# Cross-attention and feed-forward on one core: context as 128 rows and 64 paired rows, projections in front of the scores

## The chip, the cores and the metric

The kernel runs on one core of a Trainium2 chip. The metric is the time of one execution on the device in microseconds (us). One execution was also recorded by the hardware profiler; the profile and the trace below are of that one.

## What is computed

One block of a transformer on `x` (2048 rows of 256) with a context of 1601 rows of 192, in fp32. Shortened from the reference (`g_norm`, `g_out` scale the layer norms inside; all mask entries are true in the inputs, but the kernel handles any mask):

```python
q = layer_norm(layernorm(x), g_norm) @ Wq          # 16 heads of 64
k, v = split(context @ Wkv)                        # 16 heads of 64 each
k, v = concat([null_k, k]), concat([null_v, v])    # 1602 keys
sim = (q * 64**-.25) @ (k * 64**-.25).T
sim = where(mask, sim, -big)                       # null key always kept
x = x + layer_norm((softmax(sim) @ v) @ Wout, g_out)
h = [xn, -xn], xn = layernorm(x)
x = x + s2 * (2 relu(s1 * (2 relu(s0 * h @ W0)) @ W1)) @ W2    # W = +1 or -1
```

## The kernel before

The context comes transposed (192 rows, one column per key). It lies in one tile `ctx_sb` of 96 rows and two halves, so that each projection is two accumulating fp32 matmuls over 96 rows.

**Units.** The 16 heads are taken as 8 pairs `p` (64 + 64 = 128 partitions), the 2048 queries as 4 blocks `b` of 512. The main loop (L463) runs over 32 units `(p, b)`, pair outermost. The keys are cut in 13 tiles of 128 (the last of 66), and for the maxima in four chunks of 402 and 400.

**One unit**, in the order in which the loop issues it (the order is written by hand; every engine takes its own instructions in that order):

1. Scores. For each key tile, `exps` (L284) adds two 64-row matmuls, one for each head, into one of two PSUM buffers that live through the whole unit. The keys were made into steps beforehand: from tile 2 on a tile holds its difference to the tile 256 keys earlier (`keys_stepped`, L216, on POOL), so that each matmul turns the buffer into the next scores. The first two tiles also subtract a row maximum, `mT`, by a matmul with ones (L307). ACT takes the exponential (L309), POOL adds the exponentials into `acc` (L498, L500). Between the tiles stand 16 `max_chunk` (L251) of the *next* unit: TensorE makes cheaper fp32r scores from `kr` and `qr`, DVE reduces them to maxima (L262). After the last, `max_combined` (L264).
2. Values. 26 matmuls `weighted` (L312) into `av`. After the third tile, `divided` (L331) works for the *previous* unit: TensorE sums `acc` by a matmul with ones (`den`), DVE takes the reciprocal and multiplies (`aoT`, L336, L337).
3. The end of the unit: ACT copies `av` (L542). Then, in blocks 0 to 2, projections of the next pair follow: `project_v` and `project_k`, as the table `ahead` (L371) shares them out: block 0 two value groups and key chunk 0, block 1 two value groups and key chunk 1, block 2 key chunks 2 and 3 and then `keys_stepped`. Then `project_out` of the previous unit (`po`, added into `y_sb` on DVE, L329), `max_turned` of the next unit (a transpose on TensorE, then `mT` on DVE, L274), and `project_q` two units ahead (`psq`, read by ACT as `qr` and `qT`, L197 and L198).

In `project_k` DVE multiplies by the mask (`kT`, L211) and adds the null key where the mask drops one (`kr`, L212). `project_v` is read by ACT (L238); DVE puts in the null value (L242).

**PSUM** is handed out in turns from two pools of two 1024-column buffers: `spare` (the two score buffers, `av`, `po`) and `flex` (the rest). A buffer is free when its last reader is done.

**The opening** (L373 to L460) makes pair 0 itself: loads on the SP, ACT and POOL queues, the normalised input for blocks 0 and 1, all keys and values of pair 0, the first maxima. `fan` (L447), a 128x512 tile of ones times `pick`, is made there for `max_turned`. In units 0 and 1 the loop prepares the input of blocks 2 and 3 in between (L513 and L544): statistics on DVE, normalisation on ACT (`centred_beside`, L134), eight transposes on TensorE. The feed-forward layers (L566 to L656) follow the units.

Of the kernel before, what the change touches and what calls it, by code (L numbers as in the profile page):

```python
# [9 lines left out]
F32 = mybir.dt.float32  # L10
# [3 lines left out]
ALU = mybir.AluOpType  # L14
# [6 lines left out]
KEYS = M + 1  # L21
CD = 192
HEADS, DH = 16, 64
INNER = HEADS * DH
FF = 1024
NP = HEADS // 2
# [9 lines left out]
def xattn_ffn(ctx, tc, x, ctxT, mask, g_norm, null_kv, wq, wkv, wout, g_out, k0, k1, k2, s0, s1, s2, out):  # L36
    nc = tc.nc
# [8 lines left out]
    def flex(name):  # L46
        return ps_f.tile([128, 2, 512], F32, tag="f", name=name)
# [95 lines left out]
    with ExitStack() as att:  # L143
# [2 lines left out]
        ep = att.enter_context(tc.tile_pool(name="exps", bufs=KC))  # L146
        wp = att.enter_context(tc.tile_pool(name="work", bufs=2))

        ctx_sb = ap.tile([96, 2, KEYS], F32, name="ctx_sb")
        gn_sb = ap.tile([128, 2], F32, name="gn_sb")  # L150
        nullk = ap.tile([128, 1], F32, name="nullk")
        nullv = ap.tile([1, 128], F32, name="nullv")
# [3 lines left out]
        maskb = ap.tile([128, KC], F32, name="maskb")  # L156
        ones_r = ap.tile([128, 128], F32R, name="ones_r")
        mcol = ap.tile([128, 128], F32, name="mcol")
        fan = ap.tile([128, 4, 128], F32, name="fan")
        pick = ap.tile([128, 4], F32, name="pick")  # L160

        weights = {}

        def load_pair(p):
            wq_t = pp.tile([128, 2, 128], F32, tag="wq", name=f"wq_{p}")
            wkv_t = pp.tile([96, 2, 2, 128], F32, tag="wkv", name=f"wkv_{p}")
            wo_t = lp.tile([128, D], F32, tag="wo", name=f"wo_{p}")
            for kv in range(2):
                nc.sync.dma_start(
                    out=wkv_t[:, :, kv, :],  # L170
                    in_=wkv[:, ds(kv * INNER + 128 * p, 128)].rearrange("(c r) w -> r c w", c=2),
                )
                if kv == 0:
                    if p == 0:
                        load_x(0)
                    nc.sync.dma_start(out=wq_t, in_=wq[:, ts(p, 128)].rearrange("(c r) w -> r c w", c=2))
            nc.sync.dma_start(out=wo_t, in_=wout[ts(p, 128), :])
            weights[p] = (wq_t, wkv_t, wo_t)


        pairs, queries = {}, {}
# [16 lines left out]
            nc.scalar.mul(qT, ps[:, 0, :], DH**-0.5)  # L198
            queries[p, b] = (qT, qr)

        def project_k(p, n, get=flex):
            kT, _, kr = pairs[p]
            start, w = CHUNKS[n]
            keys = ds(start, w)
            ps = get(f"psk_{p}_{n}")
            for c in range(2):
                nc.tensor.matmul(  # L207
                    ps[:, 0, :w], weights[p][1][:, c, 0, :], ctx_sb[:, c, keys], start=c == 0, stop=c == 1
                )

            nc.vector.tensor_tensor(kT[:, keys], ps[:, 0, :w], keep[:, keys], ALU.mult)  # L211
            nc.vector.scalar_tensor_tensor(kr[:, keys], drop[:, keys], nullk[:, 0:1], kT[:, keys], ALU.mult, ALU.add)  # L212
            if n == 0:
                nc.vector.tensor_copy(kT[:, 0:1], nullk)

        def keys_stepped(p):  # L216

            kT = pairs[p][0]
            for at in range(256 * ((KEYS - 1) // 256), 0, -256):
                w = min(256, KEYS - at)  # L220
                nc.gpsimd.tensor_tensor(kT[:, ds(at, w)], kT[:, ds(at, w)], kT[:, ds(at - 256, w)], ALU.subtract)

        def project_v(p, n, get=flex):
            v = pairs[p][1]
            tiles = range(4 * n, min(4 * n + 4, KC))
            rows = 128 if n < 3 else KLAST
            ps = get(f"psv_{p}_{n}")
            for i, t in enumerate(tiles):
                for c in range(2):
                    nc.tensor.matmul(  # L230
                        ps[:rows, 0, ts(i, 128)],
                        ctx_sb[:, c, ds(128 * t, rows)],
                        weights[p][1][:, c, 1, :],
                        start=c == 0,
                        stop=c == 1,
                    )
            w = len(tiles)
            nc.scalar.copy(  # L238
                v[:rows, ds(4 * n, w), :], ps[:rows, 0, : 128 * w].rearrange("p (t d) -> p t d", d=128)
            )  # L240
            if n == 0:
                nc.vector.tensor_copy(v[0:1, 0, :], nullv)  # L242

# [25 lines left out]
        def max_turned(p, b):  # L269

            ps = flex(f"mt_{p}_{b}")
            nc.tensor.transpose(ps[:, 0, :128], mcol, ident)
            shifts[p, b] = wp.tile([128, 512], F32R, tag="mT", name=f"mT_{p}_{b}", bufs=1)
            nc.vector.tensor_tensor(  # L274
                shifts[p, b].rearrange("p (t q) -> p t q", t=4),
                ps[:, 0:1, :128].to_broadcast([128, 4, 128]),
                fan,
                ALU.mult,
            )

        def rows_of(k):
            return 128 if k < KC - 1 else KLAST
# [37 lines left out]
        def project_out(p, b, aoT):  # L320
            po = spare(f"po_{p}_{b}")
            pv = po.rearrange("p a (c d) -> p (a c) d", d=D)
            for t in range(4):
                nc.tensor.matmul(pv[:, t, :], aoT[:, ts(t, 128)], weights[p][2], start=True, stop=True)  # L324
            y = y_sb[:, ts(b, 4), :]
            if p == 0:
                nc.vector.tensor_copy(y, pv)
            else:
                nc.vector.tensor_tensor(y, pv, y, ALU.add)  # L329
# [38 lines left out]
        units = [(p, b) for p in range(NP) for b in range(NB)]  # L368
        extra = {0, 4, 8}

        ahead = {0: ((0, 1), (0,)), 1: ((2, 3), (1,)), 2: ((), (2, 3)), 3: ((), ())}  # L371

        begin = tc.manual_schedule()  # L373
        begin.__enter__()

        def load_x(b):
            nc.sync.dma_start(out=x_sb[:, ts(b, 4), :], in_=x[ts(b, 512), :].rearrange("(c p) d -> p c d", p=128))
# [4 lines left out]
        for n, (at, w) in enumerate(CHUNKS):  # L382
            skip = 1 if n == 0 else 0
            nc.scalar.dma_start(
                out=ctx_sb[:, :, ds(at + skip, w - skip)],
                in_=ctxT[:, ds(at + skip - 1, w - skip)].rearrange("(c r) k -> r c k", c=2),
            )
        nc.gpsimd.memset(eps2_sb, EPS * EPS)
        nc.gpsimd.memset(eps_sb, EPS)
        make_identity(nc, ident)  # L390
        nc.gpsimd.memset(keep[:, 0:1], 0)
        nc.gpsimd.memset(ctx_sb[:, :, 0:1], 0.0)
        nc.gpsimd.dma_start(out=keep[:, 1:], in_=mask.partition_broadcast(128))
        nc.gpsimd.dma_start(out=gn_sb, in_=g_norm.rearrange("(c p) -> p c", p=128))
        for j in range(2):
# [16 lines left out]
        nc.gpsimd.memset(mcol, 0.0)  # L412
        nc.gpsimd.memset(maskb, 0.0)
        nc.gpsimd.memset(ones, 1.0)
        nc.gpsimd.memset(fan, 1.0)

        nc.scalar.activation(warm, eps_sb, AF.Sqrt)

        open_pair(0)
        xn = input_root(0)  # L420
        nc.vector.tensor_scalar(ones_r, ident, 0.0, 1.0, ALU.mult, ALU.add)
        nc.vector.tensor_tensor(pick, ident[:, 0:4], ident[:, DH : DH + 4], ALU.add)
        input_normed(0, *xn)
        project_k(0, 0, slot)
        input_turned(0, slot)
        project_k(0, 1, slot)
        project_q(0, 0, slot)
        for t in range(4):
            max_chunk(0, 0, 4 * t, slot)
            if t == 1:  # L430
                project_k(0, 2, slot)
        for t in range(4):
            max_chunk(0, 0, 4 * t + 1, slot)
            if t == 1:
                project_k(0, 3, slot)
                keys_stepped(0)
        xn = input_root(1)
        input_normed(1, *xn, beside=True)
# [4 lines left out]
        nc.vector.tensor_scalar(  # L443
            maskb[:KLAST, KC - 1 : KC], mcol_u8[:KLAST, KC - 1 : KC], -MASKED, MASKED, ALU.mult, ALU.add
        )
        for t in range(4):
            nc.vector.tensor_scalar_mul(fan[:, t, :], fan[:, t, :], pick[:, t : t + 1])  # L447
        for n in (2, 3):
            for t in range(4):
                max_chunk(0, 0, 4 * t + n, slot)  # L450
                if n == 2 or t == 3:
                    if t % 2 == 1:
                        project_v(0, (0, 1)[t // 2] if n == 2 else 2, slot)
# [5 lines left out]
        project_v(0, 3)  # L459
        begin.__exit__(None, None, None)  # L460
        last = None
        with tc.manual_schedule():
            for u, (p, b) in enumerate(units):  # L463
# [232 lines left out]
```

## Time and profile before

| | us |
|---|---|
| median of 3 runs (1351.82 to 1353.6) | 1353.06 |
| the profiled execution | 1355.55 |
| its span, first to last instruction | 1353.7 |
| TensorE busy / its share | 1329.3 / 98% |
| DVE, ACT, POOL busy | 880.7, 607.7, 994.8 |
| opening, up to the first unit | 51.4 |
| the 32 units, up to the last one's first score | 1081.8 |
| mean granted TensorE clock | 0.992 |

How to read the rows shown below. Each names the line of the kernel, the engine, the operation, the tiles as out<-in, their shapes, and a count. PE is TensorE and PEld its weight loads, DVE VectorE, ACT ScalarE, POOL GpSimd, SP the queue of most loads. In a timeline the first two numbers are the start and the duration in us, with like instructions of one engine merged; in brackets stands how long the engine was idle before and what ended that. In groups, the numbers after the bar are busy us in all, mean ns of one, and idle us before. A matmul's recorded duration contains its way through the array, so neighbours overlap; the time that one costs is read from start to start.

### The profile page before, as it was taken

Reading aid. Unit: us, or ns where it says so; the run is one execution under the profiler, and the core shown is the slowest. Engines: PE = TensorE matmul, PEld = TensorE weight load, DVE = VectorE, ACT = ScalarE, POOL = GpSimd, SP = SyncE. Lnnn points to the kernel's source line nnn. Section 1 sums busy time; section 2 is a strip of 40 time slices with the busy share of each in tenths; the row PEclk is TensorE's granted clock in tenths of the full one; section 3 lists DMA queues with packets and bytes.
Section 4 is the critical chain, followed back from the end, with each engine's and each line's share of the span. In section 5 each row is a group of like instructions: output and inputs, shape, how many; then the busy total and the mean of one; then the engine's idle time right before and its main releaser. Section 6 shows DMA issues by size and latency. Waiting matters only on the chain.

```text
span 1353.7 us, 16255 instructions
## 1 busy us (share of the span) xinstructions
PE 1329.3 (98%) x6528; PEld 664.6 (49%) x6528; DVE 880.7 (65%) x957; ACT 607.7 (45%) x655; POOL 994.8 (73%) x492
## 2 busy tenths in 40 slices
PE   6999999999999999999999999999999999999998
PEld 3544444444444444444444444444444443688887
DVE  5677776676667756686767656767676884464431
ACT  1666454445444454444544454454445557421220
POOL 4377987798888987798779877987798999711100
PEclk9799999999999999999999999999999999999999
DMA  5000000000000000000000000000000010000000
GB/s 136 4 1 7 0 1 8 8 1 0 8 1 7 1 1 8 7 1 1 7 8 1 1 8 8 0 1 5 0 16 1 1 39 0 1 0 16 16 16 16
DMA packets 14940, 12.31 MB, mean 9 GB/s; under 512 B 2240, under 2 KB 14784, under 8 KB 14864
## 3 DMA queue, kind: packets, MB, share of 16 engines
q1 hardware_dynamic: 13552, 9.70, 2.5%
q10 hardware_dynamic: 832, 1.23, 0.3%
q8 instruction: 51, 0.84, 0.3%
q0 software_dynamic: 480, 0.34, 0.1%
q14 instruction: 25, 0.20, 0.1%
HBM read 9.17 MB, written 2.10 MB: 8 GB/s over the span
## 4 chain that ended last, share of the span: by engine, by line
PE 93%; DVE 3%; ACT 2%; DMA 1%; issue 0%; POOL 0%; SPq 0%; ACTq 0%
PE sT L296 28%; PE av L316 27%; PE ps L592 10%; PE max L259 8%; PE psq L196 4%; PE po L324 4%; PE psv L230 3%; PE psk L207 3%; PE ps L615 2%; PE den L334 2%; ACT e L309 1%; PE sT L307 1%; DVE mx L262 1%; DMA x_sb<-in_x 1%; PE xT L361 0%
## 5 line engine op out<-in xcount | busy, mean ns | idle before, releaser
L500 POOL TENSOR_TENSOR acc<-acc,e 128x1024 f32<-128x1024 f32 (+1 forms) x352 | 847.3, 2407 | 27.6
L262 DVE TENSOR_REDUCE mx<-max 128x2 f32<-128x800 f32 (+1 forms) x512 | 481.3, 988 | 70.9 <-PE max L259 61.2
L309 ACT ACTIVATE e<-sT,maskb 128x1024 f32<-128x1024 f32 (+1 forms) x416 | 460.0, 1115 | 64.0 <-PE sT L296 38.0
L296 PE MATMUL sT<-qT,kT 64*128 64x512 f32 (+1 forms) x1664 | 444.4, 612 | 1.6 <-ACT e L309 1.4
L316 PE MATMUL av<-e,v 128*64 128x512 f32 (+1 forms) x1664 | 369.5, 594 | 1.0
L259 PE MATMUL max<-kr,qr 64*128 64x400 f32 (+1 forms) x1024 | 285.7, 568 | 2.3 <-DVE mx L262 1.5
L316 PEld LDWEIGHTS av<-e,v 128*64 128x64 f32 (+1 forms) x1664 | 116.7, 137 | 239.0 <-issue 219.3
L259 PEld LDWEIGHTS max<-kr,qr 64*128 64x128 f32 x1024 | 97.3, 186 | 187.2 <-DVE mx L262 149.7
L296 PEld LDWEIGHTS sT<-qT,kT 64*128 64x128 f32 (+1 forms) x1664 | 135.3, 181 | 104.8 <-ACT e L309 81.5
L498 POOL TENSOR_TENSOR acc<-e,e 128x1024 f32<-128x1024 f32 x32 | 75.5, 2358 | 147.6 <-ACT e L309 147.6
L542 ACT COPY avs<-av 128x512 f32<-128x512 f32 x32 | 18.8, 587 | 327.0 <-PE av L316 327.0
L336 DVE RECIPROCAL aoT<-den 128x512 f32<-128x512 f32 x31 | 104.1, 3357 | 70.0 <-PE den L334 70.0
L197 ACT ACTIVATE qr<-psq 128x512 fp32r<-128x512 f32 x32 | 19.1, 597 | 139.1 <-PE psq L196 139.1
L592 PE MATMUL ps<-h0hi,w 128*128 128x512 f32 x256 | 79.5, 392 | 0.0
L592 PE MATMUL ps<-h0lo,w 128*128 128x512 f32 x256 | 78.9, 389 | 0.0
L211 DVE TENSOR_TENSOR kT<-psk,keep 128x400 f32<-128x400 f32 (+1 forms) x32 | 18.4, 574 | 90.0 <-PE psk L207 89.8
L119 POOL TENSOR_TENSOR y_sb<-y_sb,gout_sb 128x256 f32<-128x256 f32 x12 | 9.3, 776 | 90.1 <-DVE y_sb L86 90.1
L581 DVE SCALAR_TENSOR_TENSOR h1lo<-ps,h1hi 128x1024 fp32r<-128x1024 f32 x16 | 19.6, 1224 | 69.0 <-ACT h1hi L580 69.0
L196 PE MATMUL psq<-xnT,wq 128*128 128x512 f32 x128 | 62.2, 610 | 0.6 <-DVE kT L211 0.6
L324 PE MATMUL po<-wo,aoT 128*128 128x256 f32 x256 | 61.5, 383 | 0.0
L329 DVE TENSOR_TENSOR y_sb<-po,y_sb 128x1024 f32<-128x1024 f32 x28 | 34.2, 1220 | 40.0 <-PE po L324 39.8
L580 ACT ACTIVATE h1hi<-ps 128x1024 fp32r<-128x1024 f32 x16 | 16.4, 1027 | 94.6 <-PE ps L592 94.6
(125 smaller groups left out, 1054.8 us busy)
## 6 DMA issues: line engine op xcount, KB each, us to landing
x_sb<-in_x SPq DMA_DIRECT2D x4, 512.0 KB, 8.7
out_x<-o SPq DMA_DIRECT2D x8, 256.0 KB, 2.1
wkv<-in_wkv SPq DMA_DIRECT2D x16, 96.0 KB, 2.1
wq<-in_wq SPq DMA_DIRECT2D x8, 128.0 KB, 2.3
wo<-in_wout SPq DMA_DIRECT2D x8, 128.0 KB, 2.1
xnT<-in_k SPq DMA_DIRECT2D x1, 1024.0 KB, 5.9
ctx_sb<-in_ctxT ACTq DMA_DIRECT2D x3, 300.0 KB, 7.9
xnT<-in_k SPq DMA_DIRECT2D x1, 512.0 KB, 3.9
```

Source lines behind the costliest of these rows:

```text
L196: nc.tensor.matmul(ps[:, 0, :], weights[p][0][:, c, :], xnT[:, b, c, :], start=c == 0, stop=c == 1)
L207: nc.tensor.matmul(ps[:, 0, :w], weights[p][1][:, c, 0, :], ctx_sb[:, c, keys], start=c == 0, stop=c == 1)
L259: nc.tensor.matmul(ps[:, j, :w], queries[p, b][1][rows, ts(t, 128)], pairs[p][2][rows, ds(start, w)], start=True, stop=True)
L262: nc.vector.tensor_reduce(maxima[p, b][:, t, :, c], ps[:, :, :w], AX.X, ALU.max)
L296: nc.tensor.matmul(ps[:n, j, :], kT[rows, ds(128 * k, n)], qT[rows, :], start=k < 2, stop=k >= 2, skip_group_check=k >= 2,)
L309: nc.scalar.activation(e[:n], ps[:n], AF.Exp, bias=maskb[:n, k : k + 1])
L316: nc.tensor.matmul(av[ts(j, DH), 0, :], v[:n, k, ts(j, DH)], e[:n, j, :], start=k == 0, stop=k == KC - 1)
L324: nc.tensor.matmul(pv[:, t, :], aoT[:, ts(t, 128)], weights[p][2], start=True, stop=True)
L336: nc.vector.reciprocal(aoT, ps)
L498: nc.gpsimd.tensor_tensor(acc, es[0], es[1], ALU.add)
L500: nc.gpsimd.tensor_tensor(acc[:m], acc[:m], es[k][:m], ALU.add)
L592: nc.tensor.matmul(ps[:, f, :], w(c)[:, ts(2 * g + f, 128)], parts[part][:, c, :], start=i == 0, stop=i == len(steps) - 1,)
```

## The change

- The context is held as `ctx_a` (rows 0 to 127) and `ctx_b` (rows 128 to 191, 64 rows). `ctx_b` has the 64 rows twice, in partitions 0 to 63 and again in 64 to 127; the weights `wa`, `wb` likewise. A projection is then one matmul over 128 rows and one over 64 rows, and the 64-row ones of two chunks or tiles are issued side by side in the two halves of the array, each into its own PSUM bank.
- The opening keeps undivided matmuls for pair 0 (`first_keys`, `first_values`): `ctx_b` and `wb` have zeros in the second half there. In unit 0 the second copy of the rows is loaded, and both context tiles are multiplied by the mask once on DVE, so that keys of later pairs need no mask of their own.
- `project_k` and `project_v` make half the keys or half the values of a pair at a time: blocks 0 and 1 the keys, blocks 2 and 3 the values. They stand last in a unit, behind `max_turned`, `project_out` and `project_q`, right in front of the next unit's scores. `max_turned` comes first. `keys_stepped` runs in block 1.
- ACT writes `kT` and DVE writes `kr` straight from PSUM, each engine beginning with the other's second chunk ("crosswise"). The null key and null value columns go in on POOL.
- `fan` is gone; `mT` is the turned maxima times a broadcast `pick`.

```diff
-        ctx_sb = ap.tile([96, 2, KEYS], F32, name="ctx_sb")
+        ctx_a = ap.tile([128, KEYS], F32, name="ctx_a")
+        ctx_b = ap.tile([128, KEYS], F32, name="ctx_b")
...
-        fan = ap.tile([128, 4, 128], F32, name="fan")
-        pick = ap.tile([128, 4], F32, name="pick")
+        pick = ap.tile([128, 4, 1], F32, name="pick")
...
         def load_pair(p):
             wq_t = pp.tile([128, 2, 128], F32, tag="wq", name=f"wq_{p}")
-            wkv_t = pp.tile([96, 2, 2, 128], F32, tag="wkv", name=f"wkv_{p}")
+            wa_t = pp.tile([128, 2, 128], F32, tag="wa", name=f"wa_{p}")
+            wb_t = pp.tile([128, 2, 128], F32, tag="wb", name=f"wb_{p}")
             wo_t = lp.tile([128, D], F32, tag="wo", name=f"wo_{p}")
-            for kv in range(2):
-                nc.sync.dma_start(
-                    out=wkv_t[:, :, kv, :],
-                    in_=wkv[:, ds(kv * INNER + 128 * p, 128)].rearrange("(c r) w -> r c w", c=2),
-                )
-                if kv == 0:
-                    if p == 0:
-                        load_x(0)
-                    nc.sync.dma_start(out=wq_t, in_=wq[:, ts(p, 128)].rearrange("(c r) w -> r c w", c=2))
+            both = wkv.rearrange("r (k w) -> r k w", k=2)[:, :, ts(p, 128)]
+            nc.sync.dma_start(out=wa_t, in_=both[0:128])
+            nc.sync.dma_start(out=wb_t[:64], in_=both[128:CD])
+            if p == 0:
+                nc.gpsimd.memset(wb_t[64:], 0.0)
+                load_x(0)
+            else:
+                nc.sync.dma_start(out=wb_t[64:], in_=both[128:CD])
+            nc.sync.dma_start(out=wq_t, in_=wq[:, ts(p, 128)].rearrange("(c r) w -> r c w", c=2))
             nc.sync.dma_start(out=wo_t, in_=wout[ts(p, 128), :])
-            weights[p] = (wq_t, wkv_t, wo_t)
+            weights[p] = (wq_t, wa_t, wb_t, wo_t)
...
+        def project_k(p, m):
+            kT, _, kr = pairs[p]
+            start, w = ((0, 401), (802, 400))[m]
+            ps = flex(f"psk_{p}_{m}")
+            for i in range(2):
+                nc.tensor.matmul(
+                    ps[:, i, :w], weights[p][1][:, 0, :], ctx_a[:, ds(start + i * w, w)], start=True, stop=False
+                )
+            for i in range(2):
+                rows = ts(i, 64)
+                nc.tensor.matmul(
+                    ps[:, i, :w], weights[p][2][rows, 0, :], ctx_b[rows, ds(start + i * w, w)], start=False, stop=True
+                )
+            for i in range(2):
+                keys, other = ds(start + i * w, w), ds(start + (1 - i) * w, w)
+                nc.scalar.copy(kT[:, keys], ps[:, i, :w])
+                nc.vector.scalar_tensor_tensor(
+                    kr[:, other], drop[:, other], nullk[:, 0:1], ps[:, 1 - i, :w], ALU.mult, ALU.add
+                )
+            if m == 0:
+                nc.gpsimd.tensor_copy(kT[:, 0:1], nullk)
...
+        def first_values(n, get):
+            v = pairs[0][1]
...
+                keys = ds(128 * t, rows)
+                out_t = ps[:rows, 0, ts(i, 128)]
+                nc.tensor.matmul(out_t, ctx_a[:, keys], weights[0][1][:, 1, :], start=True, stop=False)
+                nc.tensor.matmul(out_t, ctx_b[:, keys], weights[0][2][:, 1, :], start=False, stop=True)
...
+        def project_v(p, m):
+            v = pairs[p][1]
+            ps = flex(f"psv_{p}_{m}")
+            pv = ps.rearrange("p i (t d) -> p (i t) d", d=128)
+            tiles = range(8 * m, min(8 * m + 8, KC))
+            for t in tiles:
+                n = rows_of(t)
+                nc.tensor.matmul(
+                    pv[:n, t - 8 * m, :],
+                    ctx_a[:, ds(128 * t, n)],
+                    weights[p][1][:, 1, :],
+                    start=t % 4 == 0,
+                    stop=False,
+                    skip_group_check=True,
+                )
+            for t in sorted(tiles, key=lambda t: (t % 4, t)):
+                n = rows_of(t)
+                rows = ts((t - 8 * m) // 4, 64)
+                nc.tensor.matmul(
+                    pv[:n, t - 8 * m, :],
+                    ctx_b[rows, ds(128 * t, n)],
+                    weights[p][2][rows, 1, :],
+                    start=False,
+                    stop=True,
+                    skip_group_check=True,
+                )
+            if m == 0:
+                nc.scalar.copy(v[:, 0:8, :], pv)
+                nc.gpsimd.tensor_copy(v[0:1, 0, :], nullv)
+            else:
+                nc.scalar.copy(v[:, 8:12, :], pv[:, 0:4, :])
+                nc.scalar.copy(v[:KLAST, 12, :], pv[:KLAST, 4, :])
...
-                fan,
+                pick.to_broadcast([128, 4, 128]),
...
-        ahead = {0: ((0, 1), (0,)), 1: ((2, 3), (1,)), 2: ((), (2, 3)), 3: ((), ())}
...
             nc.scalar.dma_start(
-                out=ctx_sb[:, :, ds(at + skip, w - skip)],
-                in_=ctxT[:, ds(at + skip - 1, w - skip)].rearrange("(c r) k -> r c k", c=2),
+                out=ctx_a[:, ds(at + skip, w - skip)], in_=ctxT[0:128, ds(at + skip - 1, w - skip)]
+            )
+            nc.scalar.dma_start(
+                out=ctx_b[:64, ds(at + skip, w - skip)], in_=ctxT[128:CD, ds(at + skip - 1, w - skip)]
             )
...
-        nc.gpsimd.memset(ctx_sb[:, :, 0:1], 0.0)
+        nc.gpsimd.memset(ctx_a[:, 0:1], 0.0)
+        nc.gpsimd.memset(ctx_b[:64, 0:1], 0.0)
+        nc.gpsimd.memset(ctx_b[64:], 0.0)
...
-        nc.gpsimd.memset(fan, 1.0)
...
-        project_k(0, 0, slot)
+        first_keys(0, slot)
...
-        for t in range(4):
-            nc.vector.tensor_scalar_mul(fan[:, t, :], fan[:, t, :], pick[:, t : t + 1])
...
+                if u == 0:
+                    nc.sync.dma_start(out=ctx_b[64:, 1:], in_=ctxT[128:CD, :])
+                    for part in (ctx_a, ctx_b):
+                        nc.vector.tensor_tensor(part, part, keep, ALU.mult)
...
                 if u < 2:
                     input_turned(u + 2)
-                if p + 1 < NP:
-                    for n in ahead[b][0]:
-                        project_v(p + 1, n, spare if n % 2 else flex)
-                    for n in ahead[b][1]:
-                        project_k(p + 1, n, spare if n % 2 else flex)
-                    if b == 2:
-                        keys_stepped(p + 1)
+                if nxt is not None:
+                    max_turned(*nxt)
                 if nxt is None:
                     uT = turned(0)
                 if last is not None:
                     project_out(*last[:2], aoT)
-                if nxt is not None:
-                    max_turned(*nxt)
                 if u + 2 < len(units):
                     project_q(*units[u + 2])
+                if p + 1 < NP:
+                    (project_k if b < 2 else project_v)(p + 1, b % 2)
+                    if b == 1:
+                        keys_stepped(p + 1)
                 last = (p, b, avs, acc)
```

Left out: `first_keys` and `first_values` are the former `project_k` and `project_v` with `ctx_a`, `ctx_b` and their weights over 128 rows each, called at the same places of the opening; `project_out` takes `weights[p][3]`.

More of the change, by code (lines that the diff above doesn't have):

```diff
@@ L199, in project_q, with first_keys @@
             queries[p, b] = (qT, qr)
-        def project_k(p, n, get=flex):
-            kT, _, kr = pairs[p]
+        def first_keys(n, get):
+            kT, _, kr = pairs[0]
             start, w = CHUNKS[n]
             keys = ds(start, w)
[L205 to L209, printed above, removed]
+            ps = get(f"psk_0_{n}")
+            nc.tensor.matmul(ps[:, 0, :w], weights[0][1][:, 0, :], ctx_a[:, keys], start=True, stop=False)
+            nc.tensor.matmul(ps[:, 0, :w], weights[0][2][:, 0, :], ctx_b[:, keys], start=False, stop=True)
             nc.vector.tensor_tensor(kT[:, keys], ps[:, 0, :w], keep[:, keys], ALU.mult)
@@ L221, in keys_stepped @@
                 nc.gpsimd.tensor_tensor(kT[:, ds(at, w)], kT[:, ds(at, w)], kT[:, ds(at - 256, w)], ALU.subtract)
-        def project_v(p, n, get=flex):
-            v = pairs[p][1]
+        def first_values(n, get):
+            v = pairs[0][1]
             tiles = range(4 * n, min(4 * n + 4, KC))
             rows = 128 if n < 3 else KLAST
-            ps = get(f"psv_{p}_{n}")
+            ps = get(f"psv_0_{n}")
             for i, t in enumerate(tiles):
[L229 to L236, printed above, removed]
+                keys = ds(128 * t, rows)
+                out_t = ps[:rows, 0, ts(i, 128)]
+                nc.tensor.matmul(out_t, ctx_a[:, keys], weights[0][1][:, 1, :], start=True, stop=False)
+                nc.tensor.matmul(out_t, ctx_b[:, keys], weights[0][2][:, 1, :], start=False, stop=True)
             w = len(tiles)
@@ L323, in project_out @@
             for t in range(4):
-                nc.tensor.matmul(pv[:, t, :], aoT[:, ts(t, 128)], weights[p][2], start=True, stop=True)
+                nc.tensor.matmul(pv[:, t, :], aoT[:, ts(t, 128)], weights[p][3], start=True, stop=True)
             y = y_sb[:, ts(b, 4), :]
@@ L421, in xattn_ffn @@
         nc.vector.tensor_scalar(ones_r, ident, 0.0, 1.0, ALU.mult, ALU.add)
-        nc.vector.tensor_tensor(pick, ident[:, 0:4], ident[:, DH : DH + 4], ALU.add)
+        nc.vector.tensor_tensor(pick[:, :, 0], ident[:, 0:4], ident[:, DH : DH + 4], ALU.add)
         input_normed(0, *xn)
-        project_k(0, 0, slot)
+        first_keys(0, slot)
         input_turned(0, slot)
-        project_k(0, 1, slot)
+        first_keys(1, slot)
         project_q(0, 0, slot)
@@ L430, in xattn_ffn @@
             if t == 1:
-                project_k(0, 2, slot)
+                first_keys(2, slot)
         for t in range(4):
@@ L434, in xattn_ffn @@
             if t == 1:
-                project_k(0, 3, slot)
+                first_keys(3, slot)
                 keys_stepped(0)
@@ L452, in xattn_ffn @@
                     if t % 2 == 1:
-                        project_v(0, (0, 1)[t // 2] if n == 2 else 2, slot)
+                        first_values((0, 1)[t // 2] if n == 2 else 2, slot)
                 if n == 3 and t == 1:
@@ L458, in xattn_ffn @@
         max_turned(0, 0)
-        project_v(0, 3)
+        first_values(3, flex)
         begin.__exit__(None, None, None)
```

## The prediction

> **What bounds the kernel now.** I read the page first: its busy shares, its slices, its chain.
>
> ```profile
> PE 1329.3 (98%) x6528; PEld 664.6 (49%) x6528; DVE 880.7 (65%) x957; ACT 607.7 (45%) x655; POOL 994.8 (73%) x492
> PE   6999999999999999999999999999999999999998
> PE 93%; DVE 3%; ACT 2%; DMA 1%; issue 0%; POOL 0%; SPq 0%; ACTq 0%
> PE sT L296 28%; PE av L316 27%; PE ps L592 10%; PE max L259 8%; PE psq L196 4%; PE po L324 4%; PE psv L230 3%; PE psk L207 3%; PE ps L615 2%; PE den L334 2%; ACT e L309 1%; PE sT L307 1%; DVE mx L262 1%; DMA x_sb<-in_x 1%; PE xT L361 0%
> ```
>
> TensorE is busy in every slice but the opening, and the chain is TensorE for 93% of the span. So an instruction taken off it should shorten the span, if its stage has no other limit. Next the TensorE timeline at the end of a unit (pair 4, block 0), where the edit lies; columns are start, duration, name, count:
>
> ```profile
> 643.58 3.84 PE L230 MATMUL psv<-wkv,ctx_sb 96*128 96x128 f32 x32
> 647.25 1.51 PE L207 MATMUL psk<-ctx_sb,wkv 96*128 96x402 f32 x4
> 648.61 1.89 PE L324 MATMUL po<-wo,aoT 128*128 128x256 f32 x8
> 650.34 0.27 PE L272 MATMUL mt<-ident,mcol 128*128 128x128 f32 x1
> 650.44 1.88 PE L196 MATMUL psq<-xnT,wq 128*128 128x512 f32 x4
> 652.26 1.13 PE L296 MATMUL sT<-qT,kT 64*128 64x512 f32 x4
> ```
>
> Starts follow each other with no hole: here TensorE alone sets the time. An fp32 matmul is two recorded passes (psv x32 is 8 tiles by 2 halves by 2). Now all engines at the start of the next stage, the scores:
>
> ```profile
> 613.10 1.88 PE L196 MATMUL psq<-xnT,wq 128*128 128x512 f32 x4
> 614.91 1.13 PE L296 MATMUL sT<-qT,kT 64*128 64x512 f32 x4
> 615.08 0.60 ACT L197 ACTIVATE qr<-psq 128x512 fp32r<-128x512 f32 x1 [3.22 <-PE psq L196]
> 616.38 1.11 ACT L309 ACTIVATE e<-sT,maskb 128x1024 f32<-128x1024 f32 x1 [0.21 <-PE sT L307]
> 616.50 3.69 DVE L262 TENSOR_REDUCE mx<-max 128x2 f32<-128x804 f32 x4 [1.49 <-PE max L259]
> 616.50 1.02 PE L296 MATMUL sT<-qT,kT 64*128 64x512 f32 x4
> ```
>
> The scores take 16.5 us in nearly every unit, with ACT 14.5 and DVE 14.2 to 15.2 us busy in them. So ACT and DVE almost bind there, and what matters is when the first exponential (1.47 us after the stage starts) and the first maximum (1.6 us) can begin. Last, durations by shape (busy, mean ns, idle before):
>
> ```profile
> L337 DVE TENSOR_TENSOR aoT<-avs,aoT 128x512 f32<-128x512 f32 x32 | 56.4, 1761 | 2.6
> L329 DVE TENSOR_TENSOR y_sb<-po,y_sb 128x1024 f32<-128x1024 f32 x28 | 34.2, 1220 | 40.0 <-PE po L324 39.8
> L212 DVE SCALAR_TENSOR_TENSOR kr<-drop,nullk,kT 128x400 fp32r<-128x400 uint8 x24 | 28.5, 1187 | 0.8
> L238 ACT COPY v<-psv 128x512 f32<-128x512 f32 x24 | 14.0, 585 | 31.1 <-PE psv L230 31.1
> L211 DVE TENSOR_TENSOR kT<-psk,keep 128x400 f32<-128x400 f32 x24 | 13.7, 573 | 83.9 <-PE psk L207 83.7
> ```
>
> DVE with both inputs in SBUF (L337, L212) varies from 0.64 to 2.9 us and ends as a POOL addition ends; with one input in PSUM (L211, L329) it hardly varies.
>
> **TensorE work removed.** First sT to first sT is 32.46 us for a unit without projections, 37.35 for block 0, 35.99 for block 1, 35.11 for block 2. Block 2's extra 2.65 us is two key chunks, 16/2 = 8 passes: 0.331 us a pass of 400 columns. Block 0's extra 4.89 less four key passes (1.33) leaves 3.56 for 32 value passes: 0.111; block 1 gives (3.53 - 1.33)/20 = 0.110.
> Before, a pair costs 16 key and 52 value passes. After, keys are 8 full passes and 4 slots in which the two 64-row halves run together: 12. Values are 26 full passes; eight tiles pair into 8 slots; of the last five only tiles 8 and 12 pair, so 2 + 6: 42 in all. Saved: 4 x 0.331 + 10 x 0.1105 = 2.43 us a pair, 17.0 us in the seven pairs inside the loop. Pair 0 keeps its full passes (96+96 rows become 128+128 with zeros; psk and psv passes are priced by columns).
>
> Does a pair of 64-row matmuls cost one slot? Scores are such pairs, and their two passes start within 7 ns and repeat every 0.43 us, weight loads side by side. No row shows 128-column pairs: taken at 0.11 a slot; at worst they run singly and values save nothing (7.7 us less). Two rules of the Trainium skill speak against it. "TensorEngine Tiling (Array Packing)", Tiling Modes, says that changing the tiling mode drains the engine. The trace has that price: psq's four passes of 0.43 take 1.81 until sT begins (0.10 too long), and the first sT shows 1.13 against 1.02 later; 0.21 us together. Counted as one more change in each of 28 units it would cost 5.9 us. I count none: projections now stand right ahead of the scores, so the change moves from in front of sT to inside the projection. "TensorE: Matmul & The Clock Gate", Part 1, gives about 62 ns of issue per matmul in one decode mode; a slot of two short matmuls would be 0.124 instead of 0.111, an estimate of 10 x 0.013 x 7 = 0.9 us. The trace has full passes at 55 ns per instruction, weight loads included, so I leave it to the range.
>
> **Evictions.** They now end up between projection and scores. ACT copies two key blocks (586 ns x 401/512 = 0.46 each) or one 1024-column value block (1.0, by exponentials at 1.11): ready by 1.2 us, ahead of the first exponential at 1.47. Queued behind them are the exponentials; if late, TensorE waits for the score buffers. DVE does two kr instructions. By L211 they cost 0.58 to 0.6 each, ready at 1.45; by L212, 1.19. I take the first: their operands are PSUM and one SBUF tile, like L211. Behind them is the first maximum at 1.6, then the second chunk's buffer. Cost 0, between -0.3 (queries are now evicted earlier) and +1.0 a unit. Block 2 today begins the maxima at 1.91 us and the exponentials at 1.79, and its scores last 16.55: small lateness is absorbed.
> Turning the maxima first removes exactly that lateness: 7 x 0.05 = 0.3 us gained. The turn needs the combined maxima, done about 11 us before; output projection needs aoT, ready 2 us before the values' end.
> POOL gets keys_stepped (5.3 us with gaps) one block earlier and two null columns. It finishes its sums about 2.2 us before the scores; starting the step at 1.2 us delays the next sums by under 3 us, while den reads them 19 us into the unit. Cost 0; without that slack, the delay itself.
>
> **Opening.** The four fan products (0.86 us on DVE) go; TensorE waited 1.02 us there, but ACT's value copy is next late: gain 0.5. SP issues one more load ahead of x (0.4 us) and 96 KB more (0.3 us at some 300 GB/s); ACT now issues the context in eight pieces (3.68/4 = 0.92 each), which leaves more bandwidth to x: between -1 and +0.7, taken as 0. ACT's issues end near 8 us, its first root is at 11.4. POOL gets zeroing, 1602 columns at the 0.83 ns between its 128- and 512-column clears (1.5 us), and 0.3 for weights: drop is ready at 13.9 instead of 12.1, read at 14.4; without that cover at most 1.3 us.
>
> **Unit 0.** Before the input statistics, DVE now multiplies both context tiles by the mask: two SBUF inputs, 1602 columns. From L337's shortest (0.69 for 512) one takes 1.82, plus its mean wait for POOL, 1.07: 5.8 together (3.6 to 8.1). Behind them: statistics, root, ACT's normalisation (last tile 76.3), then eight transposes at 78.9, the last needing it about 79.6. So 3.3 us are hidden: TensorE waits 2.5 plus 0.2 latency. And psq, with no output projection ahead of it in this unit, waits about 0.4 more for a PSUM buffer: 3.1 us lost (0.5 to 5.5). The second context half is loaded from SP at about 51.5 us; even at the 8.7 us of the opening's largest load it is there by 60, DVE wants it at 69. Later weight loads, one more per pair, have a whole unit.
>
> **Sum.** -17.0 - 0.3 - 0.5 + 3.1 = -14.7 us, against the profiled span of 1353.7 us (that run took 1355.55, so 1.85 lie outside). The median is 1353.06; outside time unchanged, that gives 1338.4 us. This kernel's measurement can tell about 0.2%, 2.7 us, from no change.
>
> **Rivals.**
> A (0.62): as summed, 1334 to 1343.
> B (0.12): short value pairs don't overlap: 7.7 us less, 1346. For: each has its own weight load, as long as the pass. Against: score weights load side by side.
> C (0.13): evictions delay the scores by 0.3 to 0.5 us in 28 units: 8 to 14 us given back, 1346 to 1352. For: ACT and DVE almost bind there. Against: block 2.
> D (0.09), slower: kr still waits for POOL's port. Two instructions at L212's 1.19 put the first maximum at 0.25 + 2.38 = 2.6 us, 1.0 late, in 14 units: 14 us, 1353; at its longest, 2.13, it is 2.9 late: 41 us, 1379. From 1.05 us lost per key unit it is slower. For: POOL works 73% of the span. Against: L211; the Trainium skill ("SBUF — State Buffer", Who interferes with whom) has DVE's second port shared with GpSimd, and kr now needs only one.
> E (0.04), it does not do what it says: all 64-row pairs run singly, saving 0; 1355.
>
> Range 1334 to 1348 holds A, B and most of C. Faster by over 0.2%: 0.85; within: 0.05; slower: 0.10.
>
> **What would show it.** Right: key units about 34.4 us from sT to sT, value units 35.1 and 34.5; paired passes starting in twos; kr near 0.6 us; a TensorE wait for y_sb near 82 us. Wrong: paired passes one after another (B, E); first maximum later than 2 us with scores above 16.6 (C, D); unit 0 longer than 40 us.

## The result and the profile after

The changed kernel takes 1362.6 us (median), the kernel before 1352.9: a ratio of 1.0069, 95% interval 1.0055 to 1.0083. Forecast were 1338.4 us and faster; it is slower by 0.7%. (The profile taken with that result came from an execution at a granted clock of 0.846, 1497.8 us; all readings below are from a second one at 0.993, run `changed_again`, with a span of 1360.4 us.)

Busy shares, slices and chain of the changed kernel:

```profile
PE 1306.4 (96%) x6528; PEld 655.7 (48%) x6528; DVE 831.4 (61%) x913; ACT 612.6 (45%) x676; POOL 1003.3 (74%) x508
PE   5979999999999999999999999999999999999998
PE 82%; ACT 9%; DVE 6%; issue 2%; DMA 1%; POOL 0%; ACTq 0%; SPq 0%; DVEq 0%
```

TensorE is busy for 23 us less, as it should be, and the span is 7 us longer. The chain has moved: TensorE holds 82% of it instead of 93%, ACT and DVE 15% instead of 5%. So work did leave TensorE, and waits came. The list of waits says where (who waits for whom: us in all, how often, the longest):

```profile
DVE kr L236 <- ACT kT L235: 56.6, 28, 6.4
PE max L318 <- DVE kr L236: 16.7, 14, 1.2
ACT kT L235 <- DVE kr L236: 9.8, 14, 0.7
```

TensorE waits for `kr` once in each of the 14 units that follow a key projection. The other two rows show an odd thing: `kr` waits for `kT` and `kT` waits for `kr`, though neither reads the other. The timeline of one such unit end (pair 3, block 0) shows it in order:

```profile
514.84 0.94 PE L229 MATMUL psk<-ctx_b,wb 64*128 64x401 f32 x4
515.62 1.02 PE L355 MATMUL sT<-qT,kT 64*128 64x512 f32 x4
515.86 0.49 ACT L235 COPY kT<-psk 128x401 f32<-128x401 f32 x1 [1.11 <-PE psk L229]
516.38 0.63 DVE L236 SCALAR_TENSOR_TENSOR kr<-drop,nullk,psk 128x401 fp32r<-128x401 uint8 x1 [3.28 <-ACT kT L235]
517.05 0.49 ACT L235 COPY kT<-psk 128x401 f32<-128x401 f32 x1 [0.70 <-DVE kr L236]
517.44 1.12 ACT L368 ACTIVATE e<-sT,maskb 128x1024 f32<-128x1024 f32 x1
517.58 0.63 DVE L236 SCALAR_TENSOR_TENSOR kr<-drop,nullk,psk 128x401 fp32r<-128x401 uint8 x1 [0.56 <-ACT kT L235]
518.13 1.89 DVE L321 TENSOR_REDUCE mx<-max 128x2 f32<-128x804 f32 x2
518.27 0.45 PE L318 MATMUL max<-kr,qr 64*128 64x400 f32 x2 [1.21 <-DVE kr L236]
```

Read it as a relay: ACT 0.49, DVE 0.63, ACT 0.49, DVE 0.63, each starting where the other ends. The crosswise reading does not happen; the four evictions stand in a row and end 2.6 us after the scores began. The first exponential comes at 1.82 us (1.47 before), the first maximum at 2.51 (1.6 before), and TensorE's second maxima chunk, which needs the PSUM buffer of `psk`, stands still for 1.21 us.

In unit 0, the rows of the late input (DVE, then ACT, then TensorE):

```profile
66.09 2.88 DVE L576 TENSOR_TENSOR ctx_a<-ctx_a,keep 128x1602 f32<-128x1602 f32 x1
68.89 3.98 DVE L576 TENSOR_TENSOR ctx_b<-ctx_b,keep 128x1602 f32<-128x1602 f32 x1
75.47 2.09 DVE L137 TENSOR_SCALAR nm<-mv_x 128x4 f32<-128x4 f32 x1
78.69 0.44 PE L420 MATMUL xT<-ident,y_sb 128*128 128x128 f32 x2 [2.51 <-ACT y_sb L141]
84.87 3.78 PE L199 MATMUL psq<-xnT,wq 128*128 128x512 f32 x4 [2.46 <-DVE xnT L425]
```

The two multiplications take 6.9 us, TensorE waits for the transposes' input and then for their PSUM buffer, and the query projection runs for 3.78 us instead of some 1.9: the granted clock between 79.5 and 91.1 us is 0.58.

All runs by stage, in us, cut at the starts of the first score matmul, of the first value matmul and of the first matmul behind the values of each unit (the values of units 1 to 31 take 377.3 and the rest after the last unit 191 to 192 in every run):

| run | opening | unit 0 | scores, units 1 to 31 | unit ends, 1 to 30 | span |
|---|---|---|---|---|---|
| before | 51.4 | 36.1 | 512.2 | 185.0 | 1353.7 |
| changed_again | 48.6 | 42.5 | 530.1 | 170.6 | 1360.4 |
| mask_late | 48.7 | 34.2 | 530.2 | 171.3 | 1353.0 |
| one_read | 48.4 | 42.0 | 509.9 | 171.1 | 1340.0 |
| both_mended | 49.2 | 34.2 | 509.9 | 171.5 | 1333.4 |
| mended_max_late | 49.8 | 34.2 | 510.5 | 182.9 | 1346.1 |
| two_tiles | 49.9 | 43.1 | 516.2 | 172.3 | 1350.2 |
| early | 48.8 | 43.0 | 511.1 | 181.7 | 1353.3 |
| unpaired | 49.1 | 43.2 | 540.6 | 176.9 | 1378.5 |
| before_max_first | 49.0 | 38.7 | 510.7 | 185.4 | 1352.7 |

Before to changed: opening -2.8, unit 0 +6.4, scores +17.9, unit ends -14.4, values and rest -0.4: +6.7. The unit ends gave what was forecast (2.46 us in each full pair); the scores took more than all of it back. The medians are 9.7 us apart and not 6.7: the profiled execution of the kernel before took 1355.55 us, 2.6 over its median, and its longer opening does not come from its program (`before_max_first` has the same opening, line for line, in 49.0 us).

### The profile page after: what moved, and what is told of

Same layout as the page of the kernel before. It is cut to its first block, busy times and chain, and to the rows that moved or that the text cites. A ratio compares the mean times of both kernels' runs of the same rounds, so it can differ in the third digit from the quotient of the medians.

```text
span 1495.7 us, 16271 instructions
## 1 busy us (share of the span) xinstructions
PE 1456.6 (97%) x6528; PEld 686.7 (46%) x6528; DVE 858.8 (57%) x913; ACT 622.3 (42%) x676; POOL 1000.5 (67%) x508
## 4 chain that ended last, share of the span: by engine, by line
PE 93%; DVE 3%; ACT 3%; issue 0%; DMA 0%; SPq 0%; ACTq 0%; DVEq 0%
PE av L375 27%; PE sT L355 27%; PE ps L654 11%; PE max L318 7%; PE psq L199 4%; PE po L383 4%; PE ps L677 2%; PE den L393 2%; PE psv L276 2%; PE psk L224 1%; DVE kr L236 1%; PE psv L288 1%; PE sT L366 1%; ACT kT L235 1%; PE psk L229 1%; DVE mx L321 1%
## 5 line engine op out<-in xcount | busy, mean ns | idle before, releaser
L321 DVE TENSOR_REDUCE mx<-max 128x2 f32<-128x800 f32 (+1 forms) x512 | 488.5, 989 | 135.7 <-PE max L318 134.8
L368 ACT ACTIVATE e<-sT,maskb 128x1024 f32<-128x1024 f32 (+1 forms) x416 | 463.5, 1115 | 104.6 <-PE sT L355 43.2
L355 PE MATMUL sT<-qT,kT 64*128 64x512 f32 (+1 forms) x1664 | 496.8, 675 | 0.5
L375 PE MATMUL av<-e,v 128*64 128x512 f32 (+1 forms) x1664 | 429.8, 675 | 0.1
L318 PE MATMUL max<-kr,qr 64*128 64x400 f32 (+1 forms) x1024 | 318.3, 635 | 16.4 <-DVE kr L236 14.2
L375 PEld LDWEIGHTS av<-e,v 128*64 128x64 f32 (+1 forms) x1664 | 123.8, 145 | 287.5 <-issue 267.3
L333 DVE TENSOR_TENSOR mT<-mt,pick 128x512 fp32r<-128x512 f32 x32 | 22.1, 691 | 140.8 <-PE mt L331 140.8
L654 PE MATMUL ps<-h0hi,w 128*128 128x512 f32 x256 | 86.1, 419 | 0.0
L199 PE MATMUL psq<-xnT,wq 128*128 128x512 f32 x128 | 71.6, 689 | 2.8 <-DVE xnT L425 2.8
L247 POOL TENSOR_TENSOR kT<-kT 128x256 f32<-128x256 f32 (+1 forms) x48 | 31.8, 662 | 62.1 <-ACT kT L235 45.5
L383 PE MATMUL po<-wo,aoT 128*128 128x256 f32 x256 | 69.5, 419 | 0.0
```

The source lines that it names most:

```text
L199: nc.tensor.matmul(ps[:, 0, :], weights[p][0][:, c, :], xnT[:, b, c, :], start=c == 0, stop=c == 1)
L318: nc.tensor.matmul(ps[:, j, :w], queries[p, b][1][rows, ts(t, 128)], pairs[p][2][rows, ds(start, w)], start=True, stop=True)
L321: nc.vector.tensor_reduce(maxima[p, b][:, t, :, c], ps[:, :, :w], AX.X, ALU.max)
L355: nc.tensor.matmul(ps[:n, j, :], kT[rows, ds(128 * k, n)], qT[rows, :], start=k < 2, stop=k >= 2, skip_group_check=k >= 2,)
L368: nc.scalar.activation(e[:n], ps[:n], AF.Exp, bias=maskb[:n, k : k + 1])
L375: nc.tensor.matmul(av[ts(j, DH), 0, :], v[:n, k, ts(j, DH)], e[:n, j, :], start=k == 0, stop=k == KC - 1)
```

## The experiments

Edits are against the changed kernel unless said otherwise; ratios are to the kernel before on the same chip.

**The changed kernel again** (no edit).

> The changed kernel once more, for a profile at the full clock: about 1362.6 us as measured. Theory S (a chain between ACT and DVE): in the units that follow a key projection the two evictions wait for each other in turn, ACT 0.5, DVE 0.63, ACT 0.5, DVE 0.63 us, so that the first maximum starts about 2.5 us after the scores do instead of 1.6, the first exponential about 1.8 instead of 1.47, and those scores last about 17.6 us instead of 16.5: some 14 to 17 us in 14 units. Unit 0 is about 7 us longer than planned. The rest is as predicted: key tails about 2.1 us, value tails 2.7 and 1.9 us over a tail without projection. Rival (pairs run singly): tails 0.7 to 0.9 us longer than that each and scores unchanged.

Measured 1363.4 us, ratio 1.0075 (1.0058 to 1.0093). Scores after a key projection last 17.8 us, after values 16.5 to 16.8. Ends of units are 5.83 and 5.83 (keys), 6.48 and 5.59 (values), 3.70 without a projection. The pairs do not run singly; theory S holds in nearly all its numbers (17.8 us where it had 17.6).

**One reader of the key projection.**

```diff
-                nc.scalar.copy(kT[:, keys], ps[:, i, :w])
-                nc.vector.scalar_tensor_tensor(kr[:, other], drop[:, other], nullk[:, 0:1], ps[:, 1 - i, :w], ...)
+            nc.scalar.copy(both.rearrange("p (i k) -> p i k", i=2), ps[:, :, :w])
...
+        # behind max_combined of the next unit, from SBUF
+            nc.vector.scalar_tensor_tensor(kr[:, keys], drop[:, keys], nullk[:, 0:1], kT[:, keys], ...)
```

> ACT alone reads the key projection, in one instruction over both blocks (0.9 us); DVE makes kr from SBUF in the next unit, behind the combined maxima, where it is idle; the step and the null column follow in block 2. Theory S: key units' scores fall back to about 16.5 us, 13 to 17 us less than the changed kernel: 1346 to 1349 us. Rival (DVE is late since POOL holds its port, or the scores suffer from ACT's copies): little changes, as kr now has two SBUF inputs and ACT copies as many columns; 1358 to 1365 us.

Measured 1341.9 us, ratio 0.992 (0.9902 to 0.9938): 21.5 us less than the changed kernel. The scores after keys last 16.35 us; the first exponential comes at 1.35 us and the first maximum at 1.48, 0.11 sooner than in the kernel before: behind paired passes the first score matmuls take 1.02 us, behind the query projection 1.13. 14 x (17.81 - 16.35) = 20.4 us of the gain lie in these scores. ACT copies as many columns, so its copies alone are not the cause. For `kr` this run decides less: it now has two SBUF inputs, the form that waits for POOL, but it has also left the place in front of the maxima. Its durations (below) and the next run decide that.

**A tile for each key block**, both engines still crosswise; `project_q` ahead of `project_out`.

```diff
-            ps = flex(f"psk_{p}_{m}")
+            ps = [flex(f"psk_{p}_{m}_{i}") for i in range(2)]
```

> The crosswise reading as it was, but each key block has a PSUM tile of its own; the query projection moves in front of the output projection so that the second tile is free in time. Same instructions, same banks in use. If the wait comes from both engines reading one tile (the program orders them), ACT and DVE now read at the same time: the first maximum starts about 1.6 to 1.8 us into the scores, those scores last about 16.5 us, the kernel takes 1343 to 1347 us. If the chip itself makes one engine wait for the other (a PSUM port, or POOL's port), the chain remains: 1360 to 1364 us.

Measured 1351.2 us, ratio 0.9983 (0.9975 to 0.9991): 12.2 us less than the changed kernel, but 4 us above what was expected. The timeline at the same place:

```profile
513.26 1.02 PE L355 MATMUL sT<-qT,kT 64*128 64x512 f32 x4
513.46 0.49 ACT L235 COPY kT<-psk 128x401 f32<-128x401 f32 x1 [2.80 <-PE psk L229]
513.50 1.18 DVE L236 SCALAR_TENSOR_TENSOR kr<-drop,nullk,psk 128x401 fp32r<-128x401 uint8 x2 [1.03 <-PE psk L229]
514.17 0.49 ACT L235 COPY kT<-psk 128x401 f32<-128x401 f32 x1 [0.22 <-DVE kr L236]
514.72 0.64 PE L318 MATMUL max<-kr,qr 64*128 64x402 f32 x4 [0.20 <-ACT kT L235]
```

ACT and DVE start 0.04 us apart, with the same instructions and, as before, each in a bank of its own. So the chip does not make one wait for the other, and POOL does not either; the wait belongs to the tile that both read (ACT's second copy still waits 0.22 us for DVE on the tile that they share). What was missed: two evictions now hold both `flex` buffers, so the first maxima chunk waits too (scores 16.82 us), and in unit 1 the query projection waits for its buffer (its end lasts 8.42 us instead of 6.70).

**The mask behind the statistics**; the five sign instructions go to unit 2.

```diff
                     input_normed(u + 2, *input_root(u + 2), beside=True)
                     nc.scalar.activation(warm, eps_sb, AF.Exp)
+                if u == 0:
+                    for part in (ctx_a, ctx_b):
+                        nc.vector.tensor_tensor(part, part, keep, ALU.mult)
...
-                if u == 0:
+                if u == 2:
                     nc.vector.tensor_scalar(sgn, s_sb[:, 0:2], 0.0, None, ALU.is_ge)
```

> In unit 0 the two multiplications by the mask stand behind the input statistics on DVE, and the five small sign instructions move to unit 2. If the mask's place costs what the trace suggests (TensorE waits for y_sb and for a PSUM buffer), unit 0 gets 5 to 8 us shorter and the kernel takes 1355 to 1358 us. If the loss of unit 0 lies elsewhere (the transposes, the clock after the opening), within 1 us of the changed kernel, 1362.

Measured 1355.2 us, ratio 1.0012 (1.0005 to 1.0019): 8.2 us less than the changed kernel. Unit 0 lasts 34.24 us instead of 42.52; the end of unit 2, where the sign instructions now stand, grows by 0.7 us, and nothing else moves by as much. Its query projection is back at full clock:

```profile
76.19 1.09 PE L420 MATMUL xT<-ident,y_sb 128*128 128x128 f32 x8
78.85 1.98 PE L199 MATMUL psq<-xnT,wq 128*128 128x512 f32 x4 [1.46 <-DVE xnT L425]
```

**No pairs.** Every 64-row matmul uses partitions 0 to 63.

```diff
-                rows = ts(i, 64)
+                rows = ts(0, 64)
...
-                rows = ts((t - 8 * m) // 4, 64)
+                rows = ts(0, 64)
```

> The 64-row matmuls all use partitions 0 to 63, so that none runs beside another; nothing else differs from the changed kernel. If pairs cost one slot, this costs 4 key passes of 0.331 and 10 value passes of 0.11 us in each of 7 pairs: 17 us more, 1379 to 1380 us. If the pairs run singly already (rivals B and E), it takes as long as the changed kernel, or 9 us more if only key pairs overlap. Part of the loss may hide behind the evictions' chain only if TensorE weren't the bound there; none is expected to.

Measured 1380.4 us, ratio 1.02 (1.0183 to 1.0217): 17.0 us more than the changed kernel, the predicted worth of the pairs (that it fits to the tenth is luck: the intervals leave about 2 us). Only 6 us of it show as longer unit ends; 10.5 us show as longer scores, since the next scores begin while the last 64-row pass has yet to start:

```profile
524.09 0.69 PE L355 MATMUL sT<-qT,kT 64*128 64x512 f32 x1
524.42 0.49 PE L229 MATMUL psk<-ctx_b,wb 64*128 64x401 f32 x1
```

**Both mends together.**

> The late mask (8.2 us less) and the single reader of the key projection (21.5 us less) together. If the two losses are separate, the changed kernel's 1363.4 falls by their sum to 1333.7 us, 1.4% under the kernel before. If the late mask only moves the wait (it now delays the first keys' eviction), it stays above 1337.

Measured 1334.8 us, ratio 0.9859 (0.9843 to 0.9876): 1.1 us above the sum of the two gains. The losses are separate, and this version beats both kernels, by 1.4% and 2.1%. It is 3.6 us under the forecast for the change.

**The projections early**, behind `max_turned` and ahead of `project_out` and `project_q`.

```diff
                 if nxt is not None:
                     max_turned(*nxt)
+                if p + 1 < NP:
+                    (project_k if b < 2 else project_v)(p + 1, b % 2)
+                    if b == 1:
+                        keys_stepped(p + 1)
```

> The projections stand behind the turned maxima and ahead of the output and query projections; their evictions, chain included, then run under 3.5 us of other matmuls. The array changes its tiling once more in each of 28 units. If that costs 0.2 us each time, as psq to sT did in the profile of before: 20.5 us gained in the scores, 5.7 lost, about 1348 us. If the change of tiling is free, 1342 us. If the position in front of the scores isn't what hurts, about 1363.

Measured 1355.4 us, ratio 1.0013 (1.0004 to 1.0021): 8.0 us less than the changed kernel, not 15. The scores fall to 16.5 us, so the position in front of them is what exposes the relay. The unit ends grow by 0.29, 0.29, 0.30 and 0.51 us, and the scores, which again begin behind full-width matmuls, are 0.13 longer than in `one_read`. I had counted one more change of tiling per unit; there are two, into the paired passes and out of them, and 2 x 0.21 = 0.42 us is the 0.29 + 0.13 that a key unit shows (the first score matmuls take 1.13 us again, as in the kernel before). So in the key units the price fits and the count was wrong. The 0.51 behind the second half of the values is more than that price explains and stays open. Unit 1's end is 2.0 us longer for another reason: there the key projection waits 1.46 us for the PSUM buffer of the turned input.

**The mended kernel with the maxima turned late.**

```diff
-                if nxt is not None:
-                    max_turned(*nxt)
...
                 if last is not None:
                     project_out(*last[:2], aoT)
+                if nxt is not None:
+                    max_turned(*nxt)
```

> The mended kernel with the maxima turned after the output projection, as before the change: what turning them first is worth. mT is then made after y_sb on DVE, still 2 us or more ahead of its use in units with a projection: no difference in 28 units, at most 0.3 us in each of the last three; within 1 us of the mended kernel. If turning first shortens something else (a PSUM buffer handed out in another order), more than 2 us slower.

Measured 1346.7 us, ratio 0.9946 (0.9931 to 0.9961): 11.9 us slower than the mended kernel, where I had expected no difference. From unit 3 on each of the 25 unit ends with a projection is 0.40 us longer (those of units 0, 1 and 2: 0, 0.2 and 1.1), 11.4 us in all, and the waits name the reason:

```profile
PEld psv L278 <- DVE mT L335: 13.9, 14, 2.0
PEld psk L224 <- DVE mT L335: 11.7, 13, 0.9
```

The projection takes the PSUM buffer of the turned maxima; turned late, that is freed only when DVE has done `y_sb` (1.22 us) and `mT` (0.68), after the projection could have begun.

**The kernel before, with the maxima turned first** (edit against the kernel before).

```diff
+                if nxt is not None:
+                    max_turned(*nxt)
                 if p + 1 < NP:
                     for n in ahead[b][0]:
...
-                if nxt is not None:
-                    max_turned(*nxt)
```

> The kernel before, with one part of the change alone: the maxima are turned ahead of the projections. In the changed order turning them first was worth 12 us, since the projection takes the PSUM buffer of the turned maxima and had to wait for mT. If that is the whole reason, it is worth next to nothing here, where nothing after the turn takes that buffer in a hurry: within 1 us of the kernel before, 1352 to 1353 (the prediction had 0.3 us less). If turning first helps by itself (mT ready for the scores), 3 to 10 us faster.

Measured 1353.95 us, ratio 1.0002 (0.9991 to 1.0013): no difference in total. In the trace it is a gain and a loss. From unit 2 on the unit ends are 1.4 us shorter in sum and the scores 1.5. Units 0 and 1 take 4.2 us more: `psv` now takes the PSUM buffer of the turned input and waits 1.45 us for it in each, and in the first of them the granted clock is then 0.85 (79.5 to 91.1 us; 1.00 in the kernel before). Turning first is worth 12 us only behind the new order, where it hands the projection its buffer.

## Why the prediction was wrong

- **TensorE work removed: right.** Forecast 2.43 us a pair; a full pair's unit ends fell from 26.19 to 23.73 us, 2.46 (about 0.2 of it comes from turning the maxima first, as the unit ends of `before_max_first` show). The pairs are worth 17.0 us, as `unpaired` shows. Rivals B and E fall.
- **The change of tiling: right.** The trace's 0.21 us, taken from one row, explains the key units of `early`, and it is not paid again when paired passes stand against the paired scores. An issue floor beyond it does not show.
- **Evictions at cost 0: the step that failed.** "Ready by 1.2 us" for ACT and "ready at 1.45" for DVE were each worked out alone, as if the diff's "crosswise" meant side by side. The durations were right (0.49 and 0.63); the program runs them one after another, since both read one PSUM tile. That is 1.32 us in each of 14 units in the changed kernel against the kernel before (18.5 us), and 1.46 against a version without it. The 14 units behind values lost nothing in sum (-0.9 us behind the first halves, +1.0 behind the second).

  The argument that "small lateness is absorbed" was a misreading: it took the starts, 1.91 and 1.79 us, from one unit and the length, 16.55 us, from others. The unit with those starts is that of 582.19 us (stretch, its length, then the engines' busy times; an undisturbed unit below it):

```profile
582.19:598.99 16.80, 16.72 (x90) 7.17 (x89) 15.19 (x17) 14.52 (x15) 15.50 (x11) 1.00 0.00 0
614.91:631.41 16.50, 16.45 (x90) 7.19 (x89) 14.16 (x16) 14.49 (x15) 13.18 (x7) 1.00 0.00 0
```

  0.32 us late, it lasts 0.30 us longer; the units of 16.55 us begin their maxima at 1.67, 0.08 late. Lateness was paid nearly in full already there, so the evidence held against rival C spoke for it. The profile of before also had a sign of the relay, in a row that I did not use:

```profile
DVE xnT L366 <- ACT xnT L362: 7.8, 3, 3.9
```

  There, too, ACT and DVE read two halves of one PSUM tile (the transposed input), and DVE starts when ACT ends (80.77 behind 80.74 us) although no data passes between them. They also write halves of one tile there, so this row alone does not say which tile makes the wait.
- **Rival D had the size and the wrong cause.** It put the maxima 1.0 us late at 14 us in all; they were 0.9 late, at 18.5 us. `kr` takes 630 to 633 ns in every one of 28 executions: it never waits for POOL, as its one SBUF input let expect. The changed kernel's groups, with the mean of each behind the bar:

```profile
L236 DVE SCALAR_TENSOR_TENSOR kr<-drop,nullk,psk 128x401 fp32r<-128x401 uint8 x14 | 8.8, 632 | 30.0 <-ACT kT L235 30.0
L236 DVE SCALAR_TENSOR_TENSOR kr<-drop,nullk,psk 128x400 fp32r<-128x400 uint8 x14 | 8.8, 631 | 26.5 <-ACT kT L235 26.5
```
- **Maxima first at 0.3 us: mis-sized, for one cause.** The lateness behind block 2 does go in `before_max_first` (0.75 us in seven units, not 0.3), but units 0 and 1 lose more than all the gains there, and in the new order the same move is worth 11.9 us. I asked when `mT` is needed, not who takes its buffer next.
- **Unit 0 at 3.1 us: mis-sized.** `mask_late` puts it at 8.2. The multiplications took 6.9 us instead of 5.8 (the 1.82 us taken for an undisturbed one is not 0.69 us scaled by columns, 2.16, but the shortest measured is 1.81). `nm` behind them took 2.09 instead of 0.96: with one input, too, it ends where a POOL addition ends, at 77.5 us. And behind TensorE's waits the granted clock was 0.58 from 79.5 to 91.1 us, where `mask_late`, without them, has 1.00; the slower projections I had not counted.
- **Opening at 0.5 us: not shown.** It is 1.5 to 3.0 us shorter in all eight versions of the change than in the one profile of before. But `before_max_first`, whose opening is not edited, is 2.4 us shorter too. The granted clock from 30 to 50 us goes with it: 0.50 in the profile of before, 0.50 and then 0.66 in `before_max_first`, 0.83 in the changed kernel's; x lands no sooner (9.3 and 9.1 us). So far as one profiled execution of each can tell, the difference need not come from the change.

With the forecast's other terms as they were, evictions at +18.5 instead of 0 and unit 0 at +8.2 instead of +3.1 turn -14.7 into about +9, close to the measured +9.7.

## What to carry to other kernels

When an edit puts evictions right in front of the next stage, write down each reader of each PSUM tile in program order: here two engines on one tile took turns even in different banks, and the sum of their times counted, not the longer one. When a trace seems to say that lateness is absorbed, read the start and the length in the same unit. For every step that is moved, ask which buffer it frees and who takes it next: here that made the same move worth 0 or 12 us. A saving on a saturated engine counts in full only if the stage behind it starts as early as before: compare when its first instruction on each engine begins.

## What the runs showed that was not expected

- A lone 64-row pass leaves the other half of the array free for the next operation: without pairs, a score pass starts 0.33 us before the last key pass, and 10.5 of the 17 us went into longer scores, not longer unit ends.
- Behind some 8 us of broken TensorE work in unit 0 (76.5 to 84.8 us) the query projection took 3.78 us at a granted clock of 0.50, against 1.98 us at 1.00 in `mask_late`.
- DVE with a PSUM and a SBUF input kept within 3 ns over 28 executions beside a POOL that was 74% busy; with two SBUF inputs, 1602 columns took 1.81, 2.88, 3.98 and 4.00 us, and the POOL additions beside the longer ones 3.8 to 3.9 us instead of 2.4.
